# A bidirectional selective scan on one core: channel-outermost partitions, doubled rows in DRAM, and transfers kept in program order

## The chip, the cores and the metric

One core of one Trainium2 chip runs the whole kernel. Its engines, by the names the profile uses: PE (matrix products; PEld loads its weights), DVE (vector), ACT (activation functions and copies), POOL (the second vector engine), SP (here it only issues transfers). Sixteen DMA engines move data between DRAM and the on-chip memories: SBUF, and PSUM, which holds PE's results. The metric is device microseconds for one execution, lower is better.

## The reference, cut to what matters

The program is a chain of four layers on an image tensor of 4 x 128 channels x 64 x 64 pixels. The change concerns the last layer, a selective state-space scan in both directions over the L = 4096 pixels of each image, with 256 inner channels d and 16 states n:

```
xs, z = split(in_proj(rms_norm(seq)))                 # 256 channels each
xs    = silu(causal_conv1d(xs))
dt, Bm, Cm = split(xs @ x_proj)                        # 8, 16, 16 rows
delta = softplus(dt_proj(dt))
def scan(u, delta, A, Bm, Cm, D, z):
    h_l = exp(delta_l * A) * h_(l-1) + delta_l * Bm_l * u_l   # for each (d, n)
    y_l = sum_n h_l * Cm_l + D * u_l
    return y * silu(z)
y   = scan forward + flip(scan of the flipped sequence)
out = layer_norm(out_proj(y)) + gamma * x * m          # m: a sigmoid map
```

D and z are the same in both directions, so the two are summed first: y = sum_n (h_forward + h_back) * C + 2 D u, times silu(z).

## The kernel before, in words

The layers run one after the other. Layers 0 to 2 are not touched. The last layer has two functions.

**layer3_prepare** computes, image by image, what the scan needs, and stores it in DRAM: `xs_d`, `sz_d` = silu(z), `delta_d`, `du_d` = delta * u, `xdbl_d` with the rows of B and C, and `low_d`.

**layer3_scan** works on 128 tiles: 4 images x 2 channel halves x 16 groups of 8 channels. A tile puts 8 channels x 16 states on the 128 partitions; its 4096 columns are two halves h of 2048. For tile n the work is:

- `by_channels` (L973 to L977) loads delta (`dl`) and delta*u (`du`) per half: 8 rows of DRAM, read 16 times, 1 MB on chip each. `by_states` (L958 to L970) loads B and C once per image and half.
- `inputs` (L980 on): POOL multiplies `dbu = du * B` (L985).
- `piece` (L988 on), eight times per tile: ACT makes `da = exp(delta * A)` of 1024 columns in PSUM (L997), DVE scans it (L999). Pieces e = 0 to 3 go forward through halves 0, 0, 1, 1; pieces 4 to 7 go back through halves 1, 1, 0, 0. There are six buffers h.
- `merge` (L1009 on): PE adds forward and back for a block of 512 columns, by two products with the identity into PSUM `mg` (L1014). `block_of` says which block: e = 0 to 3 are the blocks of half 1, e = 4 to 7 those of half 0.
- `copied` (L1019 on): ACT copies `mg` to `m` (L1023). `times_c`: POOL multiplies `m` by C (L1027).
- `sums` (L1029 on): PE adds the 16 states of a channel (L1036). Four tiles fill the rows of one PSUM tile y, of 4 blocks x 32 channels. `evacuate`: after each fourth tile, ACT copies it (L1046) and SP stores it to `y_d` (L1048).
- `finish` (L1050 to L1078), eight times per image, on 512 columns of all channels: loads y, xs and sz (`yx`, L1058), adds 2 D u by a product with the diagonal matrix `skip` (L1061), multiplies by silu(z) (DVE, L1062), projects (`po`, L1066), normalises (ACT L1068, PE L1070, ACT L72 and L73, DVE L1075), adds bias and `low_d` on POOL (L1076, L1077) and stores (L1078). The finishes of an image run during the next image's tiles, one each third tile, and those of the last image at the end.

The order of each engine's instructions is not simply the program's: a scheduler may hoist instructions unless `tc.keep_in_program_order` holds them, and in this kernel the loads of B and C and many loads of dl and du are hoisted. Each engine runs its own list in order, SP too; a transfer is issued when SP reaches it and what it waits for is done. The main loop over n and e interleaves the steps: merges of tile n-1 stand beside the scans of tile n.

Of the kernel before, what the change touches and what calls it, by code (L numbers as in the profile page):

```python
# [17 lines left out]
B = 4  # L18
# [729 lines left out]
def layer3_prepare(  # L748
# [4 lines left out]
    with ExitStack() as ctx:  # L753
# [29 lines left out]
        for b in range(B):  # L783
# [60 lines left out]
            for k2 in range(NB // 2):  # L844
# [11 lines left out]
                for mc in range(2):  # L856
                    u = f"{b}_{k2}_{mc}"
                    bias = dtb[:, mc : mc + 1]
                    shape = [P, 2 * BK]
                    dv = sb.tile(shape, F32, tag="dv", name=f"dv{u}")  # L860
                    for s in range(2):
                        pd = ps.tile([P, BK], F32, tag="mm", name=f"pd3_{u}_{s}")
                        nc.tensor.matmul(
                            pd, dtw[:, bass.ts(mc, P)], xd[0:DT_RANK, bass.ts(s, BK)], start=True, stop=True
                        )
                        nc.vector.tensor_scalar(dv[:, bass.ts(s, BK)], pd, bias, None, ALU.add)
                    ee = sb.tile(shape, F32, tag="ee", name=f"ee{u}")
                    nc.scalar.activation(ee, dv, AF.Abs)
                    nc.scalar.activation(ee, ee, AF.Exp, scale=-1.0)

                    uu = sb.tile(shape, F32, tag="uu", name=f"uu{u}")
                    nc.vector.tensor_scalar(uu, ee, 1.0, None, ALU.add)
                    nc.vector.scalar_tensor_tensor(ee, uu, 1.0, ee, ALU.subtract, ALU.subtract)
                    nc.scalar.activation(uu, uu, AF.Ln)
                    nc.vector.tensor_tensor(uu, uu, ee, ALU.subtract)
                    nc.vector.scalar_tensor_tensor(dv, dv, 0.0, uu, ALU.max, ALU.add)
                    nc.sync.dma_start(delta_d[b, mc, :, c2], dv)
                    du = sb.tile(shape, F32, tag="du", name=f"du{u}")
                    nc.gpsimd.tensor_tensor(du, dv, xs[mc][:, c2], ALU.mult)
                    nc.sync.dma_start(du_d[b, mc, :, c2], du)  # L880


def layer3_scan(
# [9 lines left out]
    with ExitStack() as ctx:  # L893
        cp = ctx.enter_context(tc.tile_pool(name="l4c", bufs=1))
        bc = ctx.enter_context(tc.tile_pool(name="l4bc", bufs=3))
# [6 lines left out]

        of8 = cp.tile([P, ND], F32, name="of8")
        nc.vector.tensor_reduce(of8, cm.ident.rearrange("p (n d) -> p d n", d=ND), AX.X, ALU.add)
# [5 lines left out]
        for j in range(4):  # L910
            nc.vector.tensor_copy(rows_of[:, j, ND * j : ND * (j + 1)], of8)

        a = []
        for name, src in (("af", a_log), ("ab", ab_log)):
# [5 lines left out]
            for c in range(2):  # L920
                spread = sb.tile([P, D_STATE, ND], F32, tag="spread", name=f"{name}_s{c}")
                nc.vector.tensor_tensor(
                    spread,
                    t[:, c, :].unsqueeze(2).broadcast_to([P, D_STATE, ND]),
                    of8.unsqueeze(1).broadcast_to([P, D_STATE, ND]),
# [3 lines left out]
                nc.tensor.matmul(pa, spread.rearrange("p n d -> p (n d)"), group, start=True, stop=True)  # L929
# [3 lines left out]
        d2 = cp.tile([P, 2], F32, name="d2")  # L933
        nc.sync.dma_start(d2, d_param)

        nc.vector.tensor_scalar(d2, d2, 2.0, None, ALU.mult)
        skip = cp.tile([P, 2, P], F32, name="skip")
        for c in range(2):
            nc.vector.tensor_scalar(skip[:, c, :], cm.ident, d2[:, c : c + 1], None, ALU.mult)
# [20 lines left out]
        def by_states(b, h):  # L960

            if (b, h) not in by_image:
                got = []
                for what in range(2):
                    t = bc.tile([P, HL], F32, tag="BC"[what], name=f"{'BC'[what]}{b}_{h}")
                    r = DT_RANK + D_STATE * what
                    src = xdbl_d[b, r : r + D_STATE, halves[h]]
                    nc.sync.dma_start(t, src.unsqueeze(1).broadcast_to([D_STATE, ND, HL]))
                    got.append(t)
                by_image[b, h] = got  # L970
            return by_image[b, h]

        def by_channels(src, n, h, tag, bufs):  # L973
            b, c, i = tiles[n]
            t = big.tile([P, HL], F32, tag=tag, bufs=bufs, name=f"{tag}{n}_{h}")
            rows8 = src[b, c, ND * i : ND * (i + 1), halves[h]]
            nc.sync.dma_start(t, rows8.unsqueeze(0).broadcast_to([D_STATE, ND, HL]))  # L977
            return t

        def inputs(n, h):  # L980

            b = tiles[n][0]
            du = by_channels(du_d, n, h, "du", 2)
            t = big.tile([P, HL], F32, tag="dbu", bufs=3, name=f"dbu{n}_{h}")
            nc.gpsimd.tensor_tensor(t, du, by_states(b, h)[0], ALU.mult)  # L985
# [20 lines left out]
        def block_of(e):  # L1006
            return (1, e) if e < 4 else (0, e - 4)
# [11 lines left out]
        def copied(n, e):  # L1019
            h, k = block_of(e)  # L1020
            if k == 0:
                st[n, "m", h] = big.tile([P, HL], F32, tag="m", bufs=2, name=f"m{n}_{h}")
            nc.scalar.copy(st[n, "m", h][:, bass.ts(k, BK)], st.pop((n, "mg", e)))  # L1023

        def times_c(n, h):
            m = st[n, "m", h]
            nc.gpsimd.tensor_tensor(m, m, by_states(tiles[n][0], h)[1], ALU.mult)  # L1027

        def sums(n, h):  # L1029

            j = tiles[n][2] % 4
# [3 lines left out]
            for g in range(4):  # L1035
                nc.tensor.matmul(  # L1036
                    st["y", h][32 * g : 32 * g + 32, :], rows_of[:, j, :], m[:, bass.ts(g, BK)],
                    start=(j == 0), stop=(j == 3), skip_group_check=True,
                )

        def evacuate(n, h):
            b, c, i = tiles[n]
            if i % 4 < 3:
                return
            t = sb.tile([P, BK], F32, tag="ye", name=f"ye{n}_{h}")
            nc.scalar.copy(t, st.pop(("y", h)))  # L1046
            r = 8 * (i - 3)
            nc.sync.dma_start(y_d[b, c, r : r + 32, halves[h]].rearrange("r (g w) -> g r w", g=4), t)  # L1048

        def finish(b, k):  # L1050
# [3 lines left out]
            gated = []  # L1054
            for c in range(2):
                yx = sb.tile([P, 3, BK], F32, tag="yx", name=f"yx{v}_{c}")
                for q, src in enumerate((y_d, xs_d, sz_d)):
                    nc.sync.dma_start(yx[:, q, :], src[b, c, :, ck])  # L1058
                py = ps_m.tile([P, BK], F32, tag="mg", name=f"py{v}_{c}")
                nc.tensor.matmul(py, cm.ident, yx[:, 0, :], start=True, stop=False)  # L1060
                nc.tensor.matmul(py, skip[:, c, :], yx[:, 1, :], start=False, stop=True)  # L1061
                nc.vector.tensor_tensor(yx[:, 0, :], py, yx[:, 2, :], ALU.mult)  # L1062
                gated.append(yx[:, 0, :])
            po = ps_m.tile([P, BK], F32, tag="mg", name=f"po3_{v}")
            for c in range(2):
                nc.tensor.matmul(po, ow[:, c, :], gated[c], start=(c == 0), stop=(c == 1))  # L1066
            sq = sb.tile([P, BK], F32, tag="sq4", bufs=1, name=f"sq4_{v}")
            nc.scalar.activation(sq, po, AF.Square)  # L1068
            pv = ps_m.tile([P, BK], F32, tag="mg", name=f"pvo{v}")
            nc.tensor.matmul(pv, cm.mean, sq, start=True, stop=True)  # L1070
            rs = sb.tile([P, BK], F32, tag="rs4", bufs=1, name=f"rs4_{v}")
            cm.rstd(nc, rs, pv)
            fl = sb.tile([P, BK], F32, tag="fl", name=f"fl{v}")
            nc.sync.dma_start(fl, low_d[b, :, ck])
            nc.vector.scalar_tensor_tensor(rs, po, lw, rs, ALU.mult, ALU.mult)  # L1075
            nc.gpsimd.tensor_scalar(rs, rs, lb, None, ALU.add)  # L1076
            nc.gpsimd.tensor_tensor(fl, rs, fl, ALU.add)  # L1077
            nc.sync.dma_start(out[b, :, ck], fl)  # L1078

        last = len(tiles) - 1  # L1080
        for h in range(2):
            st[0, "delta", h] = by_channels(delta_d, 0, h, "dl", 3)
            inputs(0, h)
        due = []
        for n in range(last + 3):
            for e in range(8):
                if n <= last:
                    piece(n, e)
                    if n < last and e in (3, 5):
                        h = (e - 3) // 2  # L1090
                        st[n + 1, "delta", h] = by_channels(delta_d, n + 1, h, "dl", 3)
                if 0 < n <= last + 1:
                    merge(n - 1, e)
                    if e > 0:
                        copied(n - 1, e - 1)
                if e == 0 and 1 < n:
                    copied(n - 2, 7)
                    times_c(n - 2, 0)
                if e == 1 and n < last:
                    inputs(n + 1, 0)  # L1100
                if e == 2 and 1 < n:
                    sums(n - 2, 0)
                if e == 3 and 1 < n:
                    evacuate(n - 2, 0)
                if e == 4 and 0 < n <= last + 1:
                    times_c(n - 1, 1)
                if e == 5 and n < last:
                    inputs(n + 1, 1)
                if e == 6 and 0 < n <= last + 1:
                    sums(n - 1, 1)  # L1110
                if e == 7 and 0 < n <= last + 1:
                    evacuate(n - 1, 1)
            b, at = divmod(n - 4, 32)
            if n >= 36 and at % 3 == 0 and at // 3 < NB:
                finish(b - 1, at // 3)
        for k in range(NB):
            finish(B - 1, k)
# [3 lines left out]
def kernel(ctx: ExitStack, tc: tile.TileContext, i: dict, out: bass.AP):  # L1121
# [10 lines left out]
    delta_d = dp.tile([B, 2, P, N], F32, name="delta_d")  # L1132
    du_d = dp.tile([B, 2, P, N], F32, name="du_d")
# [123 lines left out]
```

## Time and profile before

| what | value |
|---|---|
| median of 3 runs | 23034.86 us (23015.31 to 23040.28) |
| the profiled execution's own time | 23019.07 us |
| its span in the profile | 23016.9 us, 331367 instructions |
| mean granted clock of PE | 0.959 |
| first scan of tile 0 (start of the scan stage's loop) | 19697.1 us |
| first scan of tile 127 | 22884.5 us |
| scans L999 | 256 of 2290 ns and 768 of 2349 ns |
| products with C, L1027; idle of POOL just before them | 256 of 4519 ns; 644.8 us |
| products du * B, L985; idle just before | 256 of 4527 ns; 25.0 us |
| idle of DVE before a scan, released by PE's merge L1014 | 506.7 us before the first scan into an h buffer |

The page cuts the span into 40 equal slices of 575 us; the scan stage is the last six. Times are microseconds unless marked ns. A row of a timeline gives start, duration, engine, line, operation, output<-inputs and, in brackets, how long the engine had been idle and which instruction released it. "x3" marks three such instructions in one row.

### The profile page before, as it was taken

What the parts mean: (1) busy time and instruction counts of PE and PEld (TensorE: products, weight loads), DVE (VectorE), ACT (ScalarE), POOL (GpSimd) and SP (SyncE); (2) the same over time, 40 slices, a digit from 0 to 9 for tenths busy, and PEclk for the clock granted to TensorE, in tenths of its full rate; (3) what the DMA queues carried; (4) which work ended last, traced back from release to release, by engine and by line L of the source; (5) the groups of instructions that cost most, each with busy time, mean ns of one, the idle gap of its engine ahead of it and who ended that gap; (6) DMA issues with size and microseconds to landing.
All of it is one profiled execution on the core that took longest, in us unless ns stands there. A gap on an engine that the chain in (4) does not pass through costs nothing. (4 is left out here: it accounts for less than half of the span.)

```text
span 23016.9 us, 331367 instructions
## 1 busy us (share of the span) xinstructions
PE 20831.8 (91%) x146924; PEld 6589.8 (29%) x146924; DVE 19394.6 (84%) x9942; ACT 18588.3 (81%) x9372; POOL 3827.4 (17%) x1774
## 2 busy tenths in 40 slices
PE   9998999999999999999999999999997567677777
PEld 4443222222222222222222222222222222222222
DVE  7887889988989999988999899889997666777776
ACT  5666999999999999989999999999996325555554
POOL 5663000000000000000000000000000001677776
PEclk9999999999999999999999999999998776899999
DMA  0000000000000000000000000000000003788886
GB/s 12 12 5 12 3 4 4 4 4 4 3 4 4 4 2 2 4 7 4 4 3 4 4 4 3 3 3 2 3 2 32 0 5 113 190 196 190 195 190 168
DMA packets 251716, 812.07 MB, mean 35 GB/s; under 512 B 103901, under 2 KB 104805, under 8 KB 180133
## 3 DMA queue, kind: packets, MB, share of 16 engines
q1 hardware_dynamic: 249700, 782.48, 13.5%
q8 instruction: 1149, 18.83, 0.3%
q10 hardware_dynamic: 576, 8.39, 0.1%
q14 instruction: 291, 2.38, 0.0%
HBM read 662.02 MB, written 128.78 MB: 34 GB/s over the span
## 5 line engine op out<-in xcount | busy, mean ns | idle before, releaser
L422 ACT ACTIVATE aa<-a1pb,a1wn 128x4096 f32<-128x4096 f32 x2048 | 7424.7, 3709 | 378.3 <-PE a1pa L380 247.2
L422 ACT ACTIVATE aa<-a2pb,a2wn 128x4096 f32<-128x4096 f32 x2048 | 7424.2, 3710 | 235.9 <-PE a2pa L380 232.8
L429 DVE TENSOR_SCALAR da<-a1pb,a1wa 128x4096 f32<-128x4096 f32 x2048 | 4680.4, 2347 | 0.6 <-PE a1pa L380 0.4
L429 DVE TENSOR_SCALAR da<-a2pb,a2wa 128x4096 f32<-128x4096 f32 x2048 | 4680.5, 2347 | 0.1
L380 PE MATMUL a1pa<-da,a1pick 128*32 128x512 f32 x32768 | 3811.4, 594 | 247.2 <-DVE da L429 247.2
L380 PE MATMUL a2pa<-da,a2pick 128*32 128x512 f32 x32768 | 3811.1, 594 | 246.6 <-DVE da L429 246.6
L380 PE MATMUL a2pa<-aa,a2pick 128*32 128x512 f32 x32768 | 3711.7, 593 | 1.5 <-ACT aa L422 1.3
L380 PE MATMUL a1pa<-aa,a1pick 128*32 128x512 f32 x32768 | 3711.3, 593 | 1.5 <-ACT aa L422 1.3
L433 DVE SCALAR_TENSOR_TENSOR aa<-a1pb,a1wa,aa 128x4096 f32<-128x4096 f32 x512 | 2296.0, 4484 | 685.9 <-ACT aa L422 685.9
L433 DVE SCALAR_TENSOR_TENSOR aa<-a2pb,a2wa,aa 128x4096 f32<-128x4096 f32 x512 | 2296.1, 4485 | 673.4 <-ACT aa L422 673.4
L1014 PE MATMUL mg<-h,ident 128*128 128x512 f32 x4096 | 1995.2, 638 | 264.7 <-ACT m L1023 217.3
L999 DVE TENSOR_TENSOR_SCAN h<-da,h,dbu 128x1024 f32<-128x1024 f32 x768 | 1804.2, 2349 | 87.1 <-POOL dbu L985 4.4
L380 PEld LDWEIGHTS a1pa<-da,a1pick 128*32 128x32 f32 x32768 | 1014.2, 110 | 2855.1 <-issue 2132.0
L380 PEld LDWEIGHTS a2pa<-da,a2pick 128*32 128x32 f32 x32768 | 1014.4, 110 | 2853.7 <-issue 2130.9
L380 PEld LDWEIGHTS a2pa<-aa,a2pick 128*32 128x32 f32 x32768 | 1043.4, 110 | 2489.8 <-issue 2473.1
L380 PEld LDWEIGHTS a1pa<-aa,a1pick 128*32 128x32 f32 x32768 | 1042.8, 110 | 2490.3 <-issue 2477.0
L190 POOL TENSOR_TENSOR ssum<-ssum,et 128x512 f32<-128x512 f32 x960 | 1228.6, 1280 | 233.3 <-ACT et L185 166.6
L1027 POOL TENSOR_TENSOR m<-m,C 128x2048 f32<-128x2048 f32 x256 | 1156.9, 4519 | 644.8 <-ACT m L1023 353.3
L1014 PEld LDWEIGHTS mg<-h,ident 128*128 128x128 f32 x4096 | 795.8, 203 | 1512.0 <-issue 869.5
L985 POOL TENSOR_TENSOR dbu<-du,B 128x2048 f32<-128x2048 f32 x256 | 1153.2, 4527 | 25.0 <-DMA du<-du_d 25.0
L155 ACT COPY et<-pe 128x512 f32<-128x512 f32 x1024 | 595.4, 581 | 592.3 <-PE pe L153 575.6
L153 PE MATMUL pe<-q,k 128*128 128x512 f32 x2048 | 1051.1, 596 | 8.6 <-DVE mx L163 8.1
(269 smaller groups left out, 13063.8 us busy)
## 6 DMA issues: line engine op xcount, KB each, us to landing
dl<-delta_d SPq DMA_DIRECT2D x256, 1024.0 KB
du<-du_d SPq DMA_DIRECT2D x256, 1024.0 KB
xs_d<-xs SPq DMA_DIRECT2D x8, 2048.0 KB
sz_d<-sz SPq DMA_DIRECT2D x64, 256.0 KB
delta_d<-dv SPq DMA_DIRECT2D x32, 512.0 KB
du_d<-du SPq DMA_DIRECT2D x32, 512.0 KB
y_d<-ye SPq DMA_DIRECT2D x64, 256.0 KB
yx<-xs_d SPq DMA_DIRECT2D x64, 256.0 KB
```

The costliest lines, as they stand in the source:

```text
L153: nc.tensor.matmul(pe, k[:, bass.ts(j, P)], unit[u, "q"], start=True, stop=True)
L155: nc.scalar.copy(et, pe)
L190: nc.gpsimd.tensor_tensor(unit[u, "sum"], unit[u, "sum"], at, ALU.add)
L380: nc.tensor.matmul(pa[k][32 * g : 32 * g + 32, :], pick[v][:, 31 - jj : 63 - jj], d[:, bass.ts(4 * k + g, BK)], start=first, stop=False, s ...
L422: nc.scalar.activation(rows(at), view(t), AF.Abs, bias=wn[t][:, co : co + 1], scale=0.5 if half else 1.0)
L429: nc.vector.tensor_scalar(rows(dt), view(t), wa[:, t, co : co + 1], None, ALU.max)
L433: nc.vector.scalar_tensor_tensor(rows(at), view(t), wa[:, t, co : co + 1], rows(at), ALU.max, ALU.add)
L985: nc.gpsimd.tensor_tensor(t, du, by_states(b, h)[0], ALU.mult)
L999: nc.vector.tensor_tensor_scan(t[:, cols][:, s], da[:, s], st[n, "dbu", h][:, cols][:, s], 0.0 if e % 4 == 0 else st["last"], ALU.mult, AL ...
L1014: nc.tensor.matmul(pm, cm.ident, st[n, way, h][:, bass.ts(k, BK)], start=(way == 0), stop=(way == 1))
L1027: nc.gpsimd.tensor_tensor(m, m, by_states(tiles[n][0], h)[1], ALU.mult)
```

## The change

It is confined to the two functions of the last layer.

1. `delta_d` and `du_d` hold every row twice, and `layer3_prepare` stores both copies.
2. A tile's partitions are now channel by channel, 16 states each, instead of state by state. A load of dl or du reads the 16 rows (8 channels, two copies) outermost, each 8 times; a load of B or C reads the 16 rows as a whole 8 times over. The constants `of16`, `of8`, `spread` and `skip` follow.
3. All transfers of the scan's loop go through `moved`, which keeps them in program order on SP, and their places in the loop are written out. B and C have 2 buffers each instead of 3 and are loaded at those places.
4. `block_of` gives e = 6, 7, 0, 1 to the blocks of half 1 (6 and 7 in the loop round of the tile itself) and e = 2 to 5 to those of half 0. `m` has 3 buffers instead of 2. `copied`, `times_c` and `sums` move in the loop.
5. The terms 2 D u and silu(z) move from `finish` to each fourth tile: xs and sz are loaded there as 4 blocks x 32 rows (`beside_sums`), four small products with `skip` add to y, and DVE multiplies by sz (`gate`) where ACT copied before; the result goes to `y_d`.
6. `finish` is a generator, whose steps are taken at every second e. It loads the gated y and `low_d` alone; ACT adds the bias to `fl` and scales `po` into `mo`, POOL multiplies `mo * rs` and adds `fl`. One table of activation functions is preloaded at the start of the function.

The core of the diff:

```diff
-                    nc.sync.dma_start(delta_d[b, mc, :, c2], dv)
+                    for copy in range(2):
+                        nc.sync.dma_start(delta_d[b, mc, :, copy, c2], dv)
...
-        bc = ctx.enter_context(tc.tile_pool(name="l4bc", bufs=3))
+        bc = ctx.enter_context(tc.tile_pool(name="l4bc", bufs=2))
...
+        def moved(out, src):
+            tc.keep_in_program_order(nc.sync.dma_start(out, src))
+        def by_states(b, what, h):
+            if b < B and (b, what, h) not in by_image:
...
+                moved(t, src.unsqueeze(0).broadcast_to([ND, D_STATE, HL]))
...
-            rows8 = src[b, c, ND * i : ND * (i + 1), halves[h]]
-            nc.sync.dma_start(t, rows8.unsqueeze(0).broadcast_to([D_STATE, ND, HL]))
+            rows16 = src[b, c, ND * i : ND * (i + 1), :, halves[h]].rearrange("d o w -> (d o) w")
+            moved(t, rows16.unsqueeze(1).broadcast_to([2 * ND, ND, HL]))
...
-            return (1, e) if e < 4 else (0, e - 4)
+            return (0, e - 2) if 2 <= e < 6 else (1, e - 6 if e > 5 else e + 2)
...
+        def blocks_of(t, n, h):
+            b, c, i = tiles[n]
+            r = 32 * (i // 4)
+            return t[b, c, r : r + 32, halves[h]].rearrange("r (g w) -> g r w", g=4)
...
+                    nc.tensor.matmul(
+                        st["y", h][rows32, :], skip[rows32, c, q, :], st["xs", h][rows32, :],
+                        start=False, stop=True, skip_group_check=True, tile_position=(32 * g, 32 * g),
+                    )
...
+                nc.vector.tensor_tensor(t, st.pop(("y", h)), t, ALU.mult)
...
+                moved(blocks_of(y_d, n, h), st.pop(("gated", h)))
```

The new loop, by e (n is the tile whose scans run): merges of blocks e = 6, 7 of tile n and 0 to 5 of tile n-1, each copied one e later; then

```
e=0: load dl(n+1,0); [B(next image,0) in an image's last tile]; xs, sz for half 0 of tile n-3
e=1: store y half 1 of n-2; load du(n+1,1); [B(next image,1)]
e=2: m*C (n-1,1); sums (n-2,0)
e=3: du*B (n+1,0); gate (n-2,0); [C(image,0) in its second tile]
e=4: xs, sz for half 1 of tile n-2
e=5: du*B (n+1,1); sums (n-1,1)
e=6: load dl(n+1,1), du(n+2,0); gate (n-1,1); [C(image,1) in its first tile]
e=7: m*C (n-1,0); store y half 0 of n-2
e even: next step of a finish
```

xs, sz, gate and store do something in every fourth tile only.

## The prediction

> **What bounds the kernel now.** I read the 40 slices first: the change touches only the stage at the end, so I took the windows, then the stage's timeline. Window columns: us; busy time of PE, PEld, DVE, ACT and POOL; granted clock; DMA share; GB/s.
>
> ```profile
> 19536.00:19546.00 10.00, 9.51 (x23) 4.24 (x23) 3.31 (x6) 7.99 (x16) 0.00 (x0) 1.00 1.02 221
> 19700.00:19780.00 80.00, 55.39 (x136) 18.95 (x136) 72.20 (x32) 46.67 (x55) 62.95 (x14) 0.87 1.01 223
> 20000.00:20400.00 400.00, 313.77 (x818) 114.36 (x818) 318.44 (x137) 227.29 (x281) 305.24 (x68) 0.91 0.80 187
> ```
>
> No engine is full in the third row, and the DMA engines are at 0.80. 187 GB/s is 4.32 MB per tile of 23.1 us (mean distance of first scans in image 0), which agrees with the code: four loads of 1.049 MB and a quarter of two stores of 0.262 MB. The second row shows the full queue: 223 GB/s. So something waits. POOL and DVE of two tiles, with the idle time before each row in brackets:
>
> ```profile
> 21898.58 4.53 POOL L1027 TENSOR_TENSOR m<-m,C 128x2048 f32<-128x2048 f32 x1 [6.46 <-DVE h L999]
> 21903.06 9.04 POOL L985 TENSOR_TENSOR dbu<-du,B 128x2048 f32<-128x2048 f32 x2
> 21912.03 4.52 POOL L1027 TENSOR_TENSOR m<-m,C 128x2048 f32<-128x2048 f32 x1
> 21923.02 4.52 POOL L1027 TENSOR_TENSOR m<-m,C 128x2048 f32<-128x2048 f32 x1 [6.46 <-DVE h L999]
> ```
>
> ```profile
> 21896.15 2.29 DVE L999 TENSOR_TENSOR_SCAN h<-da,dbu 128x1024 f32<-128x1024 f32 x1 [3.70 <-PE mg L1014]
> 21906.33 2.29 DVE L999 TENSOR_TENSOR_SCAN h<-da,dbu 128x1024 f32<-128x1024 f32 x1 [0.50 <-PE mg L1014]
> 21920.59 2.29 DVE L999 TENSOR_TENSOR_SCAN h<-da,dbu 128x1024 f32<-128x1024 f32 x1 [4.58 <-PE mg L1014]
> 21930.77 2.29 DVE L999 TENSOR_TENSOR_SCAN h<-da,dbu 128x1024 f32<-128x1024 f32 x1 [0.50 <-PE mg L1014]
> 21954.69 2.29 DVE L999 TENSOR_TENSOR_SCAN h<-da,dbu 128x1024 f32<-128x1024 f32 x1 [4.92 <-PE mg L1014]
> 21964.80 2.29 DVE L999 TENSOR_TENSOR_SCAN h<-da,dbu 128x1024 f32<-128x1024 f32 x1 [0.50 <-PE mg L1014]
> ```
>
> POOL has four products per tile, 4 x 4.52 = 18.1, and one gap of 6.46: 24.4 us between equal rows. It is a ring. In the order of the built program, PE has y of half 0 (which waits for POOL's m of half 0) ahead of the last merge mg of half 1; ACT copies that merge to m of half 1, and POOL's next product is that m. The scan into half 1's h buffer waits for the same merge: 4.58. The other wait, 0.50, is da (1.12), copy (0.58), and last merge on one string. Without waits a half takes 9.57 (four scans of 2.26 to 2.43), a tile 19.14. The third pair shows a tile with a finish: 21930.77 to 21964.80 = 34.0 instead of 24.4, since ACT, PE and DVE run the whole normalisation in one go.
>
> First scans of images 0 to 3 and of the last tile stand at 19697.1, 20431.0, 21255.5, 22081.6 and 22884.5, the end at 23016.9: stretches of 734.0, 824.4, 826.2, 802.9 (31 tiles) and 132.4.
>
> **The change part by part.**
>
> *Merge order.* Both programs have the same order on POOL. On PE the four merges of half 1 now all stand ahead of y of half 0, so the 6.46 us gap has no cause left. What is late next: POOL 18.1, DVE 19.14, and the 0.5 string, which I give to both halves: 2 x (9.57 + 0.6) = 20.4. I take 20.4 as the engines' bound; without the strings it would be 19.1. A third m buffer costs nothing.
>
> *Bytes.* Per tile the four loads stay: 4.194 MB, 18.8 us at 223 GB/s. Their pattern of 16 distinct rows outermost, each read 8 times, is that of the B and C loads of the first row (221 GB/s), so I price the rearrangement itself at nothing. New per four tiles: xs and sz loads for both halves beside the two y stores, 6 x 0.262 = 1.573 MB, 0.393 MB a tile. Image 0 then moves 4.588 MB a tile, 20.6 us at 223. The finish loses its xs and sz loads and moves 4 x 0.262 MB per three tiles, 1.57 us a tile: 22.1. So the transfers overtake the engines.
>
> *Shape of the small transfers.* All six have four blocks outermost. Before, only the y store has that form; in the chain that ended last it stands just before the load of the same 256 KB by 128 rows:
>
> ```profile
> 22928.80 5.86 DMA y_d<-ye
> 22934.65 0.02 issue
> 22934.67 2.58 DMA yx<-y_d
> ```
>
> The window within that store shows a DMA share of 0.24 and its packets lie on four engines. A 2 KB packet took 0.084 to 0.116, so these four engines get 6 x 32 of them per four tiles, 4.0 to 5.6 us a tile, beside 32 packets of 8 KB at 0.52 to 0.59 (16.6 to 18.9): 20.6 to 24.4 a tile; with 1.07 for the finish's spread transfers 21.7 to 25.5. I take 21.5 and 22.7, near the low ends: when few packets were in flight an 8 KB packet took 0.31 instead of 0.60, so four engines that lag alone speed up. The high ends stay for the range.
>
> The Trainium skill speaks against this part: "DMA: Bandwidth & Descriptors", section "Rules for kernel authors", says that an outermost dimension of fewer than 16 confines a transfer to at most that many engines. The store above agrees (5.86 against 2.58). By that rule taken fully, with no speeding up, the tiles are 24.4 and 25.5 and the sum is the slow rival's; by the row of 223 GB/s alone it is 20.6 and 22.1. It would also put the B and C loads, now with 8 copies outermost, on 8 engines; no run here shows that form.
>
> *SP in program order.* dl of half 1 waits for ACT's last da of that buffer, and du(n+2) of half 0 stands behind it; the y store waits for the gate on DVE, and du of half 1 stands behind that. By hand these waits end 5.4 us (du) to 12 us (dl) before POOL or ACT need the data, so I price them at nothing; if the slack is gone, each tile pays the excess, up to about 5 us.
>
> *Gate, skip and finish.* Per four tiles: 8 skip matmuls of a quarter of the rows (bounds 0 to 8 x 0.60, PE has 20% idle) and two gates on DVE in place of two ACT copies, 0.67 each by the old gate's row; 0.34 a tile, hidden in DVE's waits; uncovered, 43 us in all. The finish, now in steps, leaves about 0.6 + 0.6 (ACT) + 1.2 and gaps, 2.9 us instead of the 10: a tile of three gets it, about 1 us a tile, and the transfers cover it (21.4 under 22.7).
>
> *Start, image changes, end.* B and C are no longer fetched ahead. First scan: B of half 0 stands before it, 4.7 us by 223 GB/s, or 9.5 on half the engines: +5, 19,702. Tile 0: eight transfers up to dl(1,0), 37.6, less 3.5 that overlap, and 0 to 14.4 for three B or C loads at half rate: 34 to 48, I take 41. Each image change has four loads more, 18.9 to 38, less what slack takes: 20. End: in before, finishes follow one another 8.9 us apart, since the next one's loads run ahead. Now each keeps SP's program order, loads after the previous output: 2.6 load, 2.1 matmuls, 1.2, 1.1, 1.3, 2.5 POOL, and issue, about 12.9 less overlap: the end takes 150 instead of 132.4 (range 130 to 165). The doubled stores of the stage before, 33.5 MB over 1 ms of nearly idle queues, cost 0 to 2; taken 0.
>
> **Sum.** 19,702 + (41 + 31 x 21.5) + 2 x (24 x 22.7 + 8 x 21.5 + 20) + (24 x 22.7 + 7 x 21.5 + 20) + 150 = 19,702 + 707.5 + 1473.6 + 715.3 + 150 = 22,748 of span. Before's profiled execution was 23,019.07 with a span of 23,016.9, so 22,751; the median of the runs shown was 15.8 above it. I say **22,760**.
>
> **Rivals.**
> 1. *Transfers do not bind.* Then 20.4 and 21.4, tile 0 at 35 and changes at 10: 19,702 + 667 + 2 x 687 + 666 + 150 = 22,559, some 22,575 as a median. For it: 223 GB/s was seen with the queue full, but not shown to be the ceiling in this mix. Against: 4.94 MB in 21.4 us is 231 GB/s.
> 2. *Engines 0 to 3 at their full price* (slower). 24.4 and 25.5: 19,702 + 797 + 2 x 827 + 803 + 150 = 23,106, some 23,120. It decides from an average tile of (23,017 - 19,702 - 41 - 60 - 150) / 126 = 24.3 us on. For it: four lanes with all six small transfers. Against: the speeding up.
> 3. *The ring stays,* because the copy to m still comes late, and only the finish is cheaper: 23.1 and 23.9 a tile give 19,702 + 757 + 2 x 785 + 761 + 150, some 22,955. Against: the order on PE.
> 4. *The queue runs dry* behind SP's in-order waits, 5.6 us in each tile: over 23,200.
>
> **Chances.** Forecast 0.46, rivals 0.25, 0.16, 0.08, 0.05 in this order. A measurement can tell 0.2%, 46 us, from no change. Faster: 0.46 + 0.25 + 0.08 = 0.79. Of rival 2, 0.05 lies within 46 us; slower is 0.11 + 0.05. The range takes in rivals 1 and 3 and the terms' bounds: 22,500 to 23,020.
>
> **What would show it.** In the changed profile: the 6.46 us gap on POOL before m is gone (if it stands, rival 3); distances of first scans near 21.5 in image 0 and 22.7 in images 1 to 3, waits of POOL for du and of ACT for dl, DMA share near 0.95 or with four engines always busy; near 20.4 and 21.4 with waits of DVE for mg, rival 1; near 25 with a lower share, rival 2; SP idle behind the gate, rival 4. Tile 0 near 41, image changes near 20, the end near 150. A mean tile over 24.3 us would make the sign wrong.

## The result, and the profile after

The changed kernel takes **23230.01 us** (median of 4 runs, 23223.56 to 23233.82) against 23030.49 for the kernel before beside it: ratio **1.0087**, 95% interval 1.0069 to 1.0104. It is slower by 200 us; the forecast was 270 us faster, and the time lies above the range. The profiled execution has a span of 23232.0.

The two windows that stand for a tile with its transfers, image 0 and a stretch with finishes, and two short ones of the changed kernel (us; busy PE, PEld, DVE, ACT, POOL; granted clock; DMA share; GB/s):

```profile
20118.50:20123.50 5.00, 0.10 (x1) 0.10 (x1) 0.89 (x1) 2.67 (x3) 4.36 (x2) 0.92 0.25 105
20144.00:20147.00 3.00, 1.47 (x4) 0.38 (x2) 3.00 (x3) 1.63 (x2) 3.00 (x2) 1.00 0.00 0
20000.00:20400.00 400.00, 311.06 (x864) 107.59 (x864) 317.73 (x143) 220.66 (x271) 301.25 (x67) 0.94 0.84 192
20600.00:21200.00 600.00, 456.29 (x1234) 158.91 (x1234) 437.91 (x197) 323.57 (x405) 432.48 (x108) 0.90 0.82 190
```

The queue is not full: 0.84 and 192 GB/s in image 0, hardly more than before. The first row says how that comes: a share of 0.25 is the work of four of sixteen engines, for 5 us, while the others have nothing and PE and DVE wait. In the second row the queue is empty. POOL in the same tiles, idle time in brackets:

```profile
20118.08 4.50 POOL L998 TENSOR_TENSOR dbu<-du,B 128x2048 f32<-128x2048 f32 x1 [6.92 <-DMA du<-du_d]
20123.22 4.51 POOL L998 TENSOR_TENSOR dbu<-du,B 128x2048 f32<-128x2048 f32 x1 [0.64 <-DMA du<-du_d]
20127.68 9.04 POOL L1040 TENSOR_TENSOR m<-m,C 128x2048 f32<-128x2048 f32 x2
...
20193.96 4.51 POOL L998 TENSOR_TENSOR dbu<-du,B 128x2048 f32<-128x2048 f32 x1 [7.52 <-DMA du<-du_d]
20198.44 9.00 POOL L1040 TENSOR_TENSOR m<-m,C 128x2048 f32<-128x2048 f32 x2
20214.71 4.50 POOL L998 TENSOR_TENSOR dbu<-du,B 128x2048 f32<-128x2048 f32 x1 [7.28 <-DMA du<-du_d]
```

The gap of 6.46 us before m has gone, as the prediction had it; POOL now stands before dbu, for du. The groups of the page say the same for the whole stage (idle time before the group, and its main releaser):

```profile
L998 POOL TENSOR_TENSOR dbu<-du,B 128x2048 f32<-128x2048 f32 x256 | 1155.0, 4518 | 652.7 <-DMA du<-du_d 457.8
L1010 ACT ACTIVATE da<-dl,af 128x1024 f32<-128x1024 f32 x512 | 567.4, 1116 | 864.0 <-DMA dl<-delta_d 442.1
L1040 POOL TENSOR_TENSOR m<-m,C 128x2048 f32<-128x2048 f32 x256 | 1156.8, 4523 | 316.2 <-ACT m L1036 259.4
```

POOL's idle time before m fell from 644.8 to 316.2 us; before dbu it rose from 25.0 to 652.7. The change of image has waits that the kernel before did not have:

```profile
20496.36 4.49 POOL L998 TENSOR_TENSOR dbu<-du,B 128x2048 f32<-128x2048 f32 x1 [17.68 <-DMA B<-xdbl_d]
...
20531.12 4.50 POOL L998 TENSOR_TENSOR dbu<-du,B 128x2048 f32<-128x2048 f32 x1 [25.82 <-DMA B<-xdbl_d]
```

From the starts of the scans in the traces (us; "tile" is the mean distance of first scans, over 24 tiles in the middle of an image; "change" is what the four tiles around a change of image take beyond four usual tiles of image 0, mean of three; "end" runs from the last tile's first scan to the end):

| | span | first scan | tile 0 | tile, image 0 | tile, finishes | change | end |
|---|---|---|---|---|---|---|---|
| before | 23016.9 | 19697.1 | 23.4 | 23.4 | 26.3 | -2 | 132.4 |
| after, forecast | 22748 | 19702 | 41 | 21.5 | 22.7 | 20 | 150 |
| after | 23232.0 | 19711.4 | 51.7 | 23.9 | 25.6 | 49 | 168.2 |
| merges alone | 22651.4 | 19691.9 | 23.7 | 20.5 | 22.9 | 7 | 133.0 |
| after, 128 rows | 22891.1 | 19721.7 | 50.1 | 21.8 | 22.9 | 36 | 166.0 |
| the same, order free | 22726.4 | 19682.8 | 23.5 | 22.0 | 22.7 | 35 | 88.6 |

### The profile page after: what moved, and what is told of

Same layout as the page of the kernel before. It is cut to its first block, busy times and chain, and to the rows that moved or that the text cites. A ratio compares the mean times of both kernels' runs of the same rounds, so it can differ in the third digit from the quotient of the medians.

```text
span 23232.0 us, 331827 instructions
## 1 busy us (share of the span) xinstructions
PE 20763.5 (89%) x147180; PEld 6540.6 (28%) x147180; DVE 19367.5 (83%) x9918; ACT 18583.8 (80%) x9373; POOL 3819.4 (16%) x1774
## 3 DMA queue, kind: packets, MB, share of 16 engines
q1 hardware_dynamic: 257684, 816.04, 14.4%
## 4 chain that ended last, share of the span: by engine, by line
ACT 31%; PE 29%; issue 18%; DVE 15%; DMA 6%; POOL 1%; SPq 1%; DVEq 0%; ACTq 0%; POOLq 0%
ACT aa L422 29%; DVE da L429 6%; PE a1pa L380 6%; PE a2pa L380 6%; DVE h L1012 4%; PE pe L153 4%; PE pav L196 4%; DMA dl<-delta_d 2%; PE mg L1027 2%; DVE g L702 1%; DMA fl<-low_d 1%; PE a1pc L348 1%; PE a2pc L348 1%; DMA du<-du_d 1%; PE pd L687 1%
## 5 line engine op out<-in xcount | busy, mean ns | idle before, releaser
L1027 PE MATMUL mg<-h,ident 128*128 128x512 f32 x4096 | 2111.0, 658 | 841.3 <-ACT m L1036 768.9
L998 POOL TENSOR_TENSOR dbu<-du,B 128x2048 f32<-128x2048 f32 x256 | 1155.0, 4518 | 652.7 <-DMA du<-du_d 457.8
L1010 ACT ACTIVATE da<-dl,af 128x1024 f32<-128x1024 f32 x512 | 567.4, 1116 | 864.0 <-DMA dl<-delta_d 442.1
L1040 POOL TENSOR_TENSOR m<-m,C 128x2048 f32<-128x2048 f32 x256 | 1156.8, 4523 | 316.2 <-ACT m L1036 259.4
```

Source lines behind the costliest of these rows:

```text
L998: nc.gpsimd.tensor_tensor(t, du, by_states(b, 0, h), ALU.mult)
L1027: nc.tensor.matmul(pm, cm.ident, st[n, way, h][:, bass.ts(k, BK)], start=(way == 0), stop=(way == 1))
L1040: nc.gpsimd.tensor_tensor(m, m, by_states(tiles[n][0], 1, h), ALU.mult)
```

## The experiments

Two theories stood against each other. **A**: the transfers with few blocks outermost run on few engines, and these set the tile. **B**: transfers held in program order on SP wait behind one another, and the queue runs dry.

**1. Cutting the transfers.** The small ones (`e1_small16`; the store of y is cut like the loads below), the B and C loads (`e2_bc16`), both (`e3_both16`):

```diff
-                    moved(t, blocks_of(src, n, h))
+                    for g in range(4):
+                        moved(t[32 * g : 32 * g + 32, :], blocks_of(src, n, h)[g])
...
-                moved(t, src.unsqueeze(0).broadcast_to([ND, D_STATE, HL]))
+                for d in range(ND):
+                    moved(t[D_STATE * d : D_STATE * (d + 1), :], src)
```

> The six transfers per four tiles that have 4 blocks outermost (xs, sz, y) are each cut into four of 32 rows; nothing else changes. Theory A (engines 0 to 3 carry all of these beside their share of the rest, and set the tile): a tile of image 0 falls from 24.3 us to about 22, the whole by 126 x 1.8 = 230, to about 23,000. Theory B (SP's in-order waits let the queue run dry): the tile stays near 24.3, the whole within 40 us of 23,230, or above for 18 more issues of 0.5 us per four tiles on SP.

> The B and C loads, 8 copies outermost, are each cut into eight transfers of 16 rows. Theory A (8 engines carry them): tile 0 falls from 51.7 to about 40 and each of the three image changes, some 43 us over the usual tiles, by about 20: the whole by 70 to 90, to about 23,150; tiles inside an image stay at 24.3. Theory B: the changes are late because B and C are issued late and in order, so they keep 35 or more of the 43, and the whole stays within 40 us of 23,230.

> Both cuts together. Theory A: the gains of the two add up, about 22,920 and below the kernel before. Theory B: within 60 us of 23,230.

Measured: 23101.5, 23127.9 and 23069.0 us, ratios to the kernel before 1.0035, 1.0047 and 1.0022 (intervals 1.0022 to 1.0049, 1.0032 to 1.0062, 1.0013 to 1.0031). The B and C cut did what A says at the changes of image, 49 to 23 us, and left the tile at 23.9 and tile 0 at 50.8, which A had at 40. The small cut took the time with only 1 to 5 packets in flight, called lone engines below, from 3.8 to 0.8 us a tile (counted from the packet records), but the tile of image 0 rose to 24.8, with 3.5 us of an empty queue. That looked like B, but it can't be read as either: with 18 more issues per four tiles the scheduler had ordered POOL, ACT and PE anew, which shows on POOL of `e1_small16`; where the changed kernel runs its products in pairs, m and dbu now alternate and wait for copies again:

```profile
20108.33 4.51 POOL L1040 TENSOR_TENSOR m<-m,C 128x2048 f32<-128x2048 f32 x1 [3.05 <-ACT m L1036]
20112.79 4.53 POOL L998 TENSOR_TENSOR dbu<-du,B 128x2048 f32<-128x2048 f32 x1
20125.07 4.51 POOL L1040 TENSOR_TENSOR m<-m,C 128x2048 f32<-128x2048 f32 x1 [7.75 <-ACT m L1036]
20129.52 4.53 POOL L998 TENSOR_TENSOR dbu<-du,B 128x2048 f32<-128x2048 f32 x1
```

**2. The order set free** (`e4_free`).

```diff
-            tc.keep_in_program_order(nc.sync.dma_start(out, src))
+            nc.sync.dma_start(out, src)
```

> The changed kernel without holding its transfers in program order: the scheduler places them as it did in the kernel before. Theory A: the tiles inside an image stay at 24 us or more, since engines 0 to 3 carry as much; only tile 0 and the image changes gain, some 100 us in all. Theory B: the tile falls to 22 or less and the whole to 22,950 or less.

Measured: 23040.6 us, ratio 1.0011 (1.0001 to 1.0020). The tile of image 0 is 24.6, with 4.0 us of lone engines and 0.8 of an empty queue: as A says. The first scan (20 us earlier), tile 0 (23.4), the changes (25) and the end (100.4) make the gain, which is above A's 100. Freeing the transfers also moved some instructions of the other engines: 26 of POOL's 576 and some 400 of ACT's 2208 stand elsewhere.

**3. Every engine's order held, as a control.** da, merges, copies, sums and the POOL products are wrapped in `tc.keep_in_program_order(...)`, and the products are named in the changed kernel's order: `inputs(n + 1, 0)`, `times_c(n - 2, 0)`, `times_c(n - 1, 1)` at e = 2. Then with all cuts (`f1_fixed_spread`), then with the transfers free as well.

> A control. Cutting the transfers also made the scheduler reorder POOL, ACT and PE. Here the changed kernel has its da, merges, copies, state sums and POOL products all held in the order in which the program names them, with POOL's order that of the changed kernel; its transfers are as in the changed kernel. Both theories: a tile of image 0 takes 23.5 to 25 us, four engines work alone for about 3.9 us of it, and the whole is within 100 us of 23,230.

> The control with the xs, sz and y transfers cut into 32 rows and the B and C loads cut into 16 rows; every other engine has the same order as in the control. Theory A (few engines carry the transfers with few blocks outermost): the time in which four engines work alone falls from 3.9 to under 1 us a tile, the tile of image 0 to about 22, the image changes by 20 or more each, the whole to about 22,900. Theory B (waits in SP's order): the four engines' time turns into an idle queue, the tile stays at 24 or more and the whole above 23,050.

> As the run before, with the transfers no longer held in program order on SP. Theory A alone: within 60 us of the run before, but for tile 0 and the end, which gain some 90. Theory B: the queue's idle time falls under 1 us a tile, the tile of image 0 to 21 or 22 and the whole to 22,750 or less.

Measured: 23591.1, 23527.2 and 23065.9 us (ratios 1.0247, 1.0220, 1.0018). The control failed: it was to be at 23,230. Its tile takes 28.3 us, because PE's sums of half 0 stand behind an m that POOL now reaches late, and merges and copies behind them: another ring. With the tile set by that ring the cuts could show nothing (lone engines 3.9 to 0.9 us, tile 28.3 to 28.2). These three say nothing on A, and of B only that freeing the transfers was worth 460 us under that ring (tile 28.2 to 25.7).

**4. One part alone: the merges** (`e6_merges_only`), on the kernel before. The loop's calls of merge, copied, times_c, inputs, sums and evacuate take the changed kernel's places, and

```diff
-            return (1, e) if e < 4 else (0, e - 4)
+            return (0, e - 2) if 2 <= e < 6 else (1, e - 6 if e > 5 else e + 2)
...
-                st[n, "m", h] = big.tile([P, HL], F32, tag="m", bufs=2, name=f"m{n}_{h}")
+                st[n, "m", h] = big.tile([P, HL], F32, tag="m", bufs=3, name=f"m{n}_{h}")
```

> The kernel before with the new order of merges, copies, products and sums alone, three buffers m and two for B and C; its layout, its transfers, its finish and the gating stay. If the ring on POOL is what bounds the kernel before, the gap of 6.46 us before m goes, a tile of image 0 falls from 23.4 to 21.5 or less, and the whole by 126 x 1.9 = 240, to about 22,790 (finishes still cost some 10 us each). Rival: the ring only moves to another wait, the tile stays above 23 and the whole within 50 us of the kernel before.

Measured: **22657.6 us, ratio 0.9843 (0.9826 to 0.9859)**, the fastest of all, and 572 us under the changed kernel. DVE, then POOL, of two tiles of this kernel:

```profile
20113.93 2.29 DVE L999 TENSOR_TENSOR_SCAN h<-da,dbu 128x1024 f32<-128x1024 f32 x1 [0.43 <-PE mg L1014]
20116.33 7.29 DVE L999 TENSOR_TENSOR_SCAN h<-da,h,dbu 128x1024 f32<-128x1024 f32 x3
20124.11 2.29 DVE L999 TENSOR_TENSOR_SCAN h<-da,dbu 128x1024 f32<-128x1024 f32 x1 [0.50 <-PE mg L1014]
20126.51 7.29 DVE L999 TENSOR_TENSOR_SCAN h<-da,h,dbu 128x1024 f32<-128x1024 f32 x3
20134.23 2.29 DVE L999 TENSOR_TENSOR_SCAN h<-da,dbu 128x1024 f32<-128x1024 f32 x1 [0.43 <-PE mg L1014]
```

```profile
20115.79 4.54 POOL L1027 TENSOR_TENSOR m<-m,C 128x2048 f32<-128x2048 f32 x1 [2.32 <-ACT m L1023]
20120.29 9.00 POOL L985 TENSOR_TENSOR dbu<-du,B 128x2048 f32<-128x2048 f32 x2
20129.25 4.51 POOL L1027 TENSOR_TENSOR m<-m,C 128x2048 f32<-128x2048 f32 x1
20136.08 4.54 POOL L1027 TENSOR_TENSOR m<-m,C 128x2048 f32<-128x2048 f32 x1 [2.33 <-ACT m L1023]
```

Both halves now have the short wait and none the long one: 20113.93 to 20134.23 is 20.3 us a tile. POOL's gap is 2.33 and no more than its slack.

**5. The shape alone** (`h1_rows128`), then with the order free (`h2_rows128_free`). The count, the bytes and the order on all five engines are those of the changed kernel; only the blocks' shape differs:

```diff
-            r = 32 * (i // 4)
-            return t[b, c, r : r + 32, halves[h]].rearrange("r (g w) -> g r w", g=4)
+            return t[b, c, :, bass.ts(4 * h + i // 4, BK)]
```

> The changed kernel with xs, sz and y moved as 128 rows of one block of 512 columns instead of 4 blocks of 32 rows: the same number of transfers and bytes, and the same order on every engine, but the wrong part of xs, sz and y, so that the output is not the reference's. Theory A (four engines carry these transfers): four engines work alone for under 1 us a tile instead of 3.9, the tile of image 0 falls from 24.0 to 22 or less, the whole by 250 or more, to 22,980 or less. Theory B (SP's in-order waits): the queue stands idle instead, the tile stays above 23.3 and the whole above 23,150.

> As the run before (the same wrong parts), with the transfers not held in program order. Both causes are then gone: tile of image 0 at 20.3 to 21.5 by the engines' chain of 2 x (9.57 + 0.6), the whole 22,650 or less. If the tile stays above 23 as in the run that freed the order alone (24.8), neither theory holds and the finish or the gating is to blame.

Measured: **22889.5 us, ratio 0.9943 (0.9928 to 0.9958)**, and 22733.3 us, ratio 0.9876 (0.9861 to 0.9891). The windows of `h1_rows128` beside those of the changed kernel:

```profile
20000.00:20400.00 400.00, 329.40 (x953) 111.29 (x951) 346.56 (x157) 237.91 (x292) 330.25 (x75) 0.98 0.93 211
20600.00:21200.00 600.00, 497.30 (x1412) 170.64 (x1411) 495.67 (x223) 365.69 (x457) 483.11 (x119) 0.97 0.93 213
```

The share rises from 0.84 to 0.93, the rate from 192 to 211 GB/s, lone engines fall to 0.7 us a tile, and an empty queue stays at 1.1. In image 0 three tiles of four take 20.3 us, the engines' bound. A stands; within a tile B has no part, since freeing the order leaves the tile at 22.0 and 22.7. What that brings lies at tile 0, the first scan and the end. With the order free the shape is worth as much: `e4_free` and `h2_rows128_free` have the same order on DVE, PE and POOL, and lie 307 us apart.

The last run missed its 22,650: a change still costs 35, and every fourth tile, the one with the gates, takes some 26 us. In `h1_rows128` the scans of such a tile wait longer for merges beside the two gates (L1079):

```profile
20111.26 2.29 DVE L1012 TENSOR_TENSOR_SCAN h<-da,dbu 128x1024 f32<-128x1024 f32 x1 [0.50 <-PE mg L1027]
20118.41 0.67 DVE L1079 TENSOR_TENSOR sz<-y,sz 128x512 f32<-128x512 f32 x1
20125.16 2.29 DVE L1012 TENSOR_TENSOR_SCAN h<-da,dbu 128x1024 f32<-128x1024 f32 x1 [3.83 <-PE mg L1027]
20134.76 0.67 DVE L1079 TENSOR_TENSOR sz<-y,sz 128x512 f32<-128x512 f32 x1
20137.79 2.29 DVE L1012 TENSOR_TENSOR_SCAN h<-da,dbu 128x1024 f32<-128x1024 f32 x1 [2.37 <-PE mg L1027]
```

Whether the gates or the skip products make these merges late was not taken apart.

**6. The layout** (`g2_old_layout_free`): the partitions, the single rows and the loads of the kernel before, in `e4_free`.

```diff
-                moved(t, src.unsqueeze(0).broadcast_to([ND, D_STATE, HL]))
+                moved(t, src.unsqueeze(1).broadcast_to([D_STATE, ND, HL]))
...
-            moved(t, rows16.unsqueeze(1).broadcast_to([2 * ND, ND, HL]))
+            moved(t, rows8.unsqueeze(0).broadcast_to([D_STATE, ND, HL]))
```

> The changed kernel, transfers not held, with the partitions state by state again, single rows in DRAM, and the loads in their old forms (dl and du 16 copies outermost, B and C 16 rows outermost). Against the run that freed the order alone (23,041): if the layout costs by its 8 outermost copies of B and C only, the image changes fall from 25 to about 7 us over the usual tiles, the tile stays at 24.5 to 25, and the whole is 40 to 90 lower. If dl and du themselves are slower in the new form, the tile falls by over 1 us and the whole by over 150.

Measured: 22963.2 us, ratio 0.9975 (0.9965 to 0.9985): 77 under `e4_free`. The changes fall from 25 to 1 us, the tile stays at 24.6. The order on all five engines is that of `e4_free`. So dl and du cost the same in either form, and B and C do not.

**7. The finish in steps, with the new merges** (`g4_merges_steps`): the old finish as a generator, taken at every second e.

> The kernel before with the new order of merges, and its old finish (128-row loads of y, xs and sz, gate and all) run in steps, one at every second piece. If the 9 us that a finish costs with the new merges come of running it in one go, a tile with a finish falls from 29.2 to 23 or less, the whole by 24 x 6 = 145, to about 22,510. If they are the price of its engines' time and buffers, the whole stays within 50 us of 22,658.

Measured: 22818.8 us, ratio 0.9913 (0.9898 to 0.9928): a miss, 161 slower than the merges alone. Tiles of 20.3, 20.3 and 29 became about 20.3, 23 to 29 and 27 to 33, and the end grew from 133 to 186. Whether the steps' waits for their loads or their places on ACT and PE cause it was not taken apart.

## Why the prediction was wrong, point by point

**What bounds the kernel before: right.** The new order, with a third buffer m, gives 365 us by itself (22657.6 against 23022.3 for the kernel before beside it). The engines' bound of 20.4 us was measured at 20.3.

**The bytes: counted right.** With the spread shape image 0 moves its 4.59 MB a tile in 21.8 us, at 211 GB/s; the sum had 20.6 at 223. That a full queue of spread transfers would set the tile is not shown: three tiles of four took the engines' 20.3.

**The shape of the small transfers: the step that failed.** The prediction worked out 20.6 to 24.4 and 21.7 to 25.5 us for the four engines, and then said: "I take 21.5 and 22.7, near the low ends". Measured: 23.9 and 25.6. The mis-sized term is the 2 KB packet. It was priced at 0.084 to 0.116, from the kernel before, where only the y stores have that form; with six such transfers it took 0.142 in the mean over image 0. Four engines have 48 of them a tile, 6.8 us instead of 4.0 to 5.6. With 32 packets of 8 KB, some 8 while they lag alone at 0.34 and 24 at 0.58, that is 6.8 + 2.8 + 13.9 = 23.5 of 23.9 us, an estimate: these engines are busy nearly all the time. The speeding up that the choice leaned on is real (0.34 against 0.58), but helps only for the quarter of the large packets that runs alone. Exchanging the shape alone gave 341 us back. That is rival 2, given 0.16, with its 23,106 of span. Its 24.4 us came near partly by luck: it had 5.6 + 18.9, where 6.8 + 16.7 was measured, so that the dear small packets and the speeding up nearly cancel.

**Start, image changes, end: right in kind, too small.** Over rival 2's sum the span has 126 us more: the first scan 9, tile 0 11, three changes 3 x 29 = 87, the end 18, together 125. The changes are the B and C loads, by form and by place: 23 us instead of 49 when cut to 16 rows, 25 with the order free, 1 with the old forms as well. The end is the program order: outputs 14.4 us apart, against 8.9 before, and 100.4 us in all with the order free.

**SP in program order, priced at nothing: right within a tile, wrong at the ends.** With the spread shape, freeing it is worth 156 us: of the span's 165, 39 before the first scan, 27 in tile 0, 77 at the end.

**Gate and skip: priced too low.** The prediction had 0.34 us a tile, covered by DVE's waits. With the spread shape a tile with gates takes some 26 us instead of 20.3, about 1.5 a tile.

**The rearrangement, priced at nothing:** right for dl and du, wrong for B and C.

**Two slips in the sums, of no weight.** The mean distance of image 0 is 734.0 / 32 = 22.9 us, not 23.1. Rival 3's terms add up to some 778 and 755, not 785 and 761.

From the changed kernel to the merges alone, 572 us: the shape 341, the order 156, the rest 75. The rest is a balance, and that it lies near the 77 of experiment 6 is chance: against `h2_rows128_free` the merges alone gain 101 us in all in the tiles around the changes and 41 in image 0, and lose 44 at the end and 23 elsewhere. (Differences between runs of different comparisons are uncertain by some 10 us: the kernel before had medians of 23019.5 to 23030.5 in them.) The Trainium skill's rule was on this side. "DMA: Bandwidth & Descriptors", section "Rules for kernel authors", covers both forms; the share of 0.25 shows it for four blocks, and stretches with eight packets in flight (19,706 to 19,711 us of the changed kernel) for eight copies. The prediction quoted it and then chose against it.

## What to carry to other kernels

Count the work of the busiest DMA engine, not of sixteen: here a few small transfers with four blocks outermost set the pace of all the large ones behind them. Where such a count gives a bound close to the time before, and one end of it is slower, take the packet's price from the row with the most of these transfers in flight. Test a shape by exchanging it for one with the same count of instructions: a cut changes what the scheduler sees, and with it every engine's order.

## What the runs showed of the hardware that was not expected

While B or C is loaded with 8 copies outermost, the transfers beside it slow down too. At its start and at a change of image the changed kernel has the DMA engines full (share 1.02, the number behind the clock), at half the rate:

```profile
19690.00:19702.00 12.00, 0.00 (x0) 0.00 (x0) 0.00 (x0) 0.00 (x0) 0.00 (x0) 0.50 1.02 122
20496.00:20508.00 12.00, 2.64 (x9) 0.71 (x10) 4.64 (x2) 0.00 (x0) 8.95 (x2) 0.59 1.02 110
```

The kernel before at its start, where dl and du are loaded without B and C:

```profile
19690.00:19702.00 12.00, 0.00 (x0) 0.00 (x0) 4.64 (x2) 1.28 (x2) 4.81 (x2) 0.50 1.01 221
```

Its loads of B and C, with 16 rows outermost, moved 221 GB/s as well (the first row of the prediction). The median 8 KB packet of the two windows of the changed kernel took 1.1 and 1.25 us, instead of 0.6. Cut into eight transfers of 16 rows the loads still show packets of 0.94 to 0.98, so it isn't only the number of engines; in the old layout (experiment 6) 7 of 2345 packets around the first change of image took over 0.9. Which resource the eight copies share was not settled.
